# A rewritten beginning: batch 1's tokens loaded at once, its norm shared by VectorE and GpSimd, a fourth unit's queries ahead of the main loop

## The chip, the cores and the metric

The kernel runs on one core of one Trainium2 chip. The metric is the device time of one execution in microseconds, the median of several. A profiled execution gives the time line of each engine: TensorE (PE, with PEld for its weight loads), VectorE (DVE), ScalarE (ACT), GpSimd (POOL) and SyncE (SP), which only issues DMAs. DMAs are also issued by ScalarE and GpSimd, in the order of their own instructions.

## The reference

Two layers of a transformer block over x of 4 batches x 512 tokens x 320, in fp32. Each layer has self attention with 20 heads of 16, cross attention to a context of 1601 tokens of 192, and a gated feed-forward part; each of the three has a layer norm ahead of it and a residual behind it.

```
h1 = _ln(x, n1_g, n1_b)
x = _attn(h1, h1, q1, k1, v1, o1_w, o1_b, heads) + x
h2 = _ln(x, n2_g, n2_b)
x = _attn(h2, context, q2, k2, v2, o2_w, o2_b, heads) + x
h3 = _ln(x, n3_g, n3_b)
a, g = jnp.split(h3 @ ff_w1 + ff_b1, 2, axis=-1)
ff = a * gelu(g) @ ff_w2 + ff_b2
return ff + x
```

`_attn` is softmax(q k^T / 4) v per head, and `_ln` subtracts the mean and multiplies by the reciprocal root of the variance plus 1e-5.

## The kernel before, in words

**Units.** Attention is cut into units: one batch and a group of four heads, so five units per batch and attention (the first unit is batch 0, heads 0 to 3). A unit passes through these stages, and its tiles have these names:

- The norm of its batch, once for five units. VectorE makes the statistics (`st`, `mv`) of four tiles of 128 tokens and starts the reciprocal root by a guess (`root`, four instructions of `guess_root` and three rounds of `better_root`). `plain` writes the rows (`hturned`: x minus mean, times root, three instructions to a tile), TensorE transposes them into `hps`, twelve products against the unit matrix, and `turn` copies them out with gain and bias (`hT`). Behind it `biased` adds the output bias `brow` to x on GpSimd, four additions to a batch.
- `both`: queries and keys of a unit, in two halves of 256 tokens on TensorE (`qkps<-hT,wqk`; the page counts 24 passes for each half). ScalarE copies them to `halves` (for the first unit with VectorE, for others with GpSimd's `split`, a cast and a subtraction, into a high and a low part), and DMAs move them to `kT` and `q`.
- `values`: four chunks of 128 tokens for 8 heads, then four for 12 heads (`vps<-wv,hT`), copied by ScalarE into `vals`.
- The row maxima of the scores: 16 tiles of 128x512 to a unit (`sps<-kT,q`), each reduced by VectorE into `nmax`. `max_pairs` lists them in two deques of four entries, two tiles to an entry, and `round_of` sends what it is given, here four tiles at a time. `max_reduce` and `max_end` finish: three short VectorE instructions, the last of which writes `turned`, and four DMAs to `nrows`.
- The main loop's rounds, four to a unit of self attention: scores once more (`st`), with the row maximum subtracted by a product with `nrows`, the exponential on ScalarE (`pr`), the product with the values (`av`), whose copy `vo` GpSimd adds to `o`.

**Order.** Every engine works off its instructions in the order in which the program was written. In the main loop a planner sets that order: chains of small steps (`norm`, `proj`, `values` and others) with costs and due times in rounds, and `give` adds maxima of coming units. While `start["on"]` is true, at the beginning, nothing is planned: the order is written out by hand in the last part of the kernel, with `run(chain)` for the next step of a chain, `until`, `at_once` (a unit's products and moves) and `round_of`. There the DMAs use the queues of SyncE and ScalarE.

**PSUM.** There are eight banks. `bank` picks the one that is expected to be free first, from running guesses of each engine's time (`written`, `busy`), so TensorE waits for whoever reads the bank that its next product gets.

**DMA counters.** A DMA that lands counts up one of eight landing counters, which all queues share in turn. A DMA waits, before it is issued, for the landing of the one that used its counter before.

The lines of the profile that matter: L182 token loads, L226 bias loads, L523 to L539 root, L563 and L564 statistics, L627 rows, L641 transposes, L647 and L649 `hT`, L620 bias additions, L912 queries and keys, L829 and L830 the split, L880 moves of `kT` and `q`, L1039 and L1021 values, L1080 maxima's products, L1091 their reductions, L1167 and L1175 `turned` and the rows of maxima, L1328 scores, L1338 the exponential, L1354 `av`.

Of the kernel before, what the change touches and what calls it, by code (L numbers as in the profile page):

```python
# [13 lines left out]
ALU = mybir.AluOpType  # L14
# [9 lines left out]
P = 128  # L24
# [54 lines left out]
def kernel(ctx: ExitStack, tc: tile.TileContext, x, context, ws, out):  # L79
# [96 lines left out]

    def load_x(b):

        src = x[b].rearrange("(c p) d -> p c d", p=P)

        def part(t):
            dma(out=xs[b][:, t], in_=src[:, t])  # L182
            loaded[b] = clock["round"] if t == NQ - 1 else 1 << 30

        return [lambda t=t: part(t) for t in range(NQ)]
# [38 lines left out]

    def load_row(t, v):
        dma(out=t, in_=v.rearrange("(o d) -> o d", o=1).to_broadcast([P, D]))  # L226

    def load_bias(l, i):
        if i > 2:
            l, i = l + 1, i - 3  # L230
        if l < L:
            load_row(brow[(3 * l + i) % 2], ws[l][("o1_b", "o2_b", "ff_b2")[i]])

# [298 lines left out]
    def better_root(h, y, z):  # L532


        eng = nc.vector if start["on"] else nc.gpsimd
        eng.tensor_tensor(z, y, y, ALU.mult)
        eng.tensor_tensor(z, z, h, ALU.mult)
        eng.tensor_scalar(z, z, 1.5, None, ALU.add)
        eng.tensor_tensor(y, y, z, ALU.mult)  # L539
# [13 lines left out]
    def add_norm(l, b, i, put, done, due):  # L553
# [68 lines left out]
        def plain(t):  # L622
            if t == 0:
                s["hn"] = one.tile([P, DB, NQ, SLOT], F32, tag="hturned", name="hturned").rearrange("p k t w -> p (k t w)")
            for k, at, n in HK:
                w = n // SLOT
                (nc.vector if start["on"] else nc.gpsimd).tensor_scalar(  # L627
                    s["hn"][:, t * D + at : t * D + at + n].rearrange("p (d k) -> p k d", k=w),
# [7 lines left out]
        def turn(k, at, n):  # L636
            if k == 0:
                place()
            ps = bank("hps")
            for t in range(NQ):  # L640
                nc.tensor.transpose(ps[:n, t * P : (t + 1) * P], s["hn"][:, t * D + at : t * D + at + n], ident)  # L641
            written(0.5, ps)
            busy("act", 0.7, ps)
            to = s["hT"][:n, k].rearrange("p (i t w) -> p t i w", t=NQ, w=SLOT)
            src = ps[:n].rearrange("p (t i w) -> p t i w", t=NQ, w=SLOT)
            if start["on"] and k == 1:
                nc.vector.tensor_scalar(to, src, lng[i][:n, k : k + 1], lnb[i][:n, k : k + 1], ALU.mult, ALU.add)  # L647
# [508 lines left out]
    def max_end(u):  # L1156
# [14 lines left out]
        def rows():  # L1171
            for i in range(P // SLOT):
                part = slice(i * SLOT, (i + 1) * SLOT)
                queue = (nc.sync, nc.scalar, nc.gpsimd, nc.sync)[i] if start["on"] else nc.sync
                queue.dma_start(out=slots[:, :, part], in_=turned[part, :])  # L1175
# [510 lines left out]

    take_rooms(0)
    now(load_x(0))
    now(load_self(0))
    load_bias(0, 0)  # L1690
    load_bias(0, 1)
    now(load_x(1))

    add_norms(0)
    add_proj(units[0])
    warm(5)
    until(lambda: not chains["proj"], "proj")
# [4 lines left out]
    run("proj")  # L1702
    for _ in range(2 * NQ + 2):
        run("norm")
    at_once(units[1])
    add_proj(units[2])
    first = units[0]
    first.pairs = max_pairs(first)
    for chain in ("proj", "proj", "values", None):
        round_of(first.pairs[0].popleft()[1] + first.pairs[1].popleft()[1])  # L1710
        if chain:
            run(chain)

    at_once(units[2])
    run("values")
    max_reduce(first)
    max_end(first)
    loads.extend(load_x(2))
    for fs in (load_out(0, "o1_w"), load_x(3), load_cross(0)):
        loads.extend(fs)  # L1720
    second = units[1]
    second.pairs = max_pairs(second)
    for _ in range(2):
        round_of(second.pairs[0].popleft()[1] + second.pairs[1].popleft()[1])
        run("values")
        run("values")
    start["on"] = False
    clock["credit"] = 0.0

    for u in units[3:SOON]:  # L1730
        add_proj(u)
# [46 lines left out]
```

## Time and profile before

| | us |
|---|---|
| median of 3 runs (lowest, highest) | 2907.66 (2905.47, 2910.71) |
| the profiled execution | 2907.47 |
| its span on the core | 2905.7 |
| mean granted TensorE clock | 0.996 |
| first `st` on TensorE | 44.99 |
| first exponential on ScalarE | 45.99 |

In the timeline a row gives the start, the time from the first start to the last end of the merged instructions, engine, line, operation, tile written and tiles read, the shape, how many, and in brackets the idle time of the engine ahead of it and what ended it. In the windows by stage a row gives the stretch, its length, each engine's busy time with the number of instructions in brackets, the granted TensorE clock, the share of the DMA engines and what they moved.

### The profile page before, as it was taken

What the parts mean: (1) busy time and instruction counts of PE and PEld (TensorE: products, weight loads), DVE (VectorE), ACT (ScalarE), POOL (GpSimd) and SP (SyncE); (2) the same over time, 40 slices, a digit from 0 to 9 for tenths busy, and PEclk for the clock granted to TensorE, in tenths of its full rate; (3) what the DMA queues carried; (4) which work ended last, traced back from release to release, by engine and by line L of the source; (5) the groups of instructions that cost most, each with busy time, mean ns of one, the idle gap of its engine ahead of it and who ended that gap; (6) DMA issues with size and microseconds to landing.
All of it is one profiled execution on the core that took longest, in us unless ns stands there. A gap on an engine that the chain in (4) does not pass through costs nothing.

```text
span 2905.7 us, 83278 instructions
## 1 busy us (share of the span) xinstructions
PE 2847.9 (98%) x35018; PEld 1540.6 (53%) x35018; DVE 1975.7 (68%) x3752; ACT 1949.3 (67%) x4033; POOL 1301.6 (45%) x1409
## 2 busy tenths in 40 slices
PE   8999999999999999999999999999999999999999
PEld 4455555555555555355554555555555555544554
DVE  7776878888888878323257678888878878862221
ACT  3777678888888888501138776788888888893000
POOL 3656345555645555211125653455465564551100
PEclk9999999999999999999999999999999999999999
DMA  3443234232232112200113432222221122122000
GB/s 107 117 118 99 59 83 103 59 80 67 51 93 70 47 54 63 85 17 11 39 44 87 111 97 67 68 64 51 54 73 42 49 73 61 45 68 64 23 22 12
DMA packets 163495, 188.59 MB, mean 65 GB/s; under 512 B 61989, under 2 KB 109105, under 8 KB 163121
## 3 DMA queue, kind: packets, MB, share of 16 engines
q1 hardware_dynamic: 162616, 181.69, 24.6%
q8 instruction: 275, 4.51, 0.6%
q10 hardware_dynamic: 472, 1.58, 0.2%
q14 instruction: 100, 0.81, 0.1%
q0 software_dynamic: 32, 0.00, 0.0%
HBM read 55.76 MB, written 29.36 MB: 29 GB/s over the span
## 4 chain that ended last, share of the span: by engine, by line
PE 87%; DVE 6%; POOL 3%; DMA 1%; issue 1%; ACT 1%; SPq 1%; ACTq 0%; POOLq 0%; DVEq 0%
PE av L1354 22%; PE st L1328 20%; PE fps L1439 10%; PE sps L1080 8%; PE yps L1546 6%; PE vps L1039 5%; PE ops L1254 4%; PE kps L976 3%; PE qkps L912 3%; DVE nmax L1091 3%; PE fps L1499 3%; PE qps L951 2%; DVE pm L1091 2%; PE sps L1105 1%; POOL o L1374 1%
## 5 line engine op out<-in xcount | busy, mean ns | idle before, releaser
L1338 ACT ACTIVATE pr<-st 128x512 f32<-128x512 f32 (+1 forms) x2720 | 1404.9, 603 | 313.2 <-PE st L1328 283.0
L1091 DVE TENSOR_REDUCE pm<-sps 128x1 f32<-128x512 f32 (+1 forms) x1920 | 1148.9, 661 | 235.3 <-PE sps L1080 230.8
L1374 POOL TENSOR_TENSOR o<-o,vo 128x512 f32<-128x512 f32 x576 | 740.7, 1286 | 913.7 <-ACT vo L1373 889.8
L1080 PE MATMUL sps<-kT,q 32*128 32x450 f32 (+1 forms) x4800 | 860.6, 419 | 11.0 <-DMA q<-halves 5.0
L1328 PE MATMUL st<-q,kT 32*128 32x512 f32 (+1 forms) x5120 | 784.4, 419 | 1.9 <-ACT o L1368 1.5
L1354 PE MATMUL av<-pr,vals 128*32 128x512 f32 (+1 forms) x5440 | 735.2, 606 | 28.7 <-ACT pr L1338 6.2
L1328 PEld LDWEIGHTS st<-q,kT 32*128 32x128 f32 (+1 forms) x5120 | 446.6, 180 | 282.1 <-issue 113.6
L1328 PE MATMUL st<-nrows,ones 32*128 32x512 f32 (+1 forms) x2720 | 559.9, 398 | 2.9 <-DMA nrows<-turned 2.8
L1091 DVE TENSOR_REDUCE nmax<-sps 128x1 f32<-128x512 f32 x640 | 397.2, 682 | 117.3 <-PE sps L1080 113.3
L1080 PEld LDWEIGHTS sps<-kT,q 32*128 32x128 f32 x4800 | 429.6, 183 | 64.3 <-ACT pr L1338 11.5
L1373 ACT COPY vo<-av 128x512 f32<-128x512 f32 x576 | 352.5, 612 | 16.6 <-PE av L1354 8.7
L1510 ACT ACTIVATE gl<-fps,b 128x512 f32<-128x512 f32 x80 | 54.8, 687 | 408.8 <-PE fps L1499 299.1
L1439 PE MATMUL fps<-hT,w 128*128 128x512 f32 x640 | 283.1, 597 | 0.0
L1354 PEld LDWEIGHTS av<-pr,vals 128*32 128x32 f32 (+1 forms) x5440 | 111.2, 108 | 302.4 <-DVE pm L1091 187.8
L1328 PEld LDWEIGHTS st<-nrows,ones 32*128 32x128 f32 (+1 forms) x2720 | 262.3, 180 | 12.7 <-DMA nrows<-turned 3.7
L1511 DVE SCALAR_TENSOR_TENSOR hid<-fps,b,gl 128x512 f32<-128x512 f32 x80 | 59.7, 748 | 249.2 <-ACT gl L1510 247.1
L1439 PEld LDWEIGHTS fps<-hT,w 128*128 128x128 f32 x640 | 119.2, 190 | 155.1 <-issue 153.2
L1546 PE MATMUL yps<-w,hid 128*128 128x320 f32 x640 | 175.7, 434 | 0.0
L1546 PEld LDWEIGHTS yps<-w,hid 128*128 128x128 f32 x640 | 120.5, 190 | 56.3 <-ACT gl L1510 5.3
L1254 PEld LDWEIGHTS ops<-wo,aT 112*32 112x32 f32 (+1 forms) x3072 | 98.7, 110 | 67.4 <-issue 33.6
L1254 PE MATMUL ops<-wo,aT 112*32 112x160 f32 (+1 forms) x3072 | 125.7, 301 | 4.2 <-POOL aT L1236 4.0
L1115 DVE TENSOR_REDUCE pm<-sps 128x4 f32<-128x508 f32 x160 | 99.0, 681 | 39.8 <-PE sps L1105 38.8
(89 smaller groups left out, 2449.7 us busy)
## 6 DMA issues: line engine op xcount, KB each, us to landing
kT<-stages SPq DMA_DIRECT2D x80, 400.5 KB
oway<-o SPq DMA_DIRECT2D x80, 256.0 KB
q<-halves SPq DMA_DIRECT2D x80, 256.0 KB
q<-halves SPq DMA_DIRECT2D x27, 512.0 KB
kT<-halves SPq DMA_DIRECT2D x40, 256.0 KB
aT<-oway SPq DMA_DIRECT2D x32, 224.0 KB
rT<-rway SPq DMA_DIRECT2D x32, 224.0 KB
hT<-hturned SPq DMA_DIRECT2D x96, 64.0 KB
```

Of the source, the lines that this page charges most:

```text
L1039: nc.tensor.matmul(ps[f : f + m, :w], lhsT=u.kvT[:n, k, at + f : at + f + m], rhs=wv[:n, k, h0 * DH : h1 * DH], start=(k == 0), stop=(k == ...
L1080: nc.tensor.matmul(own[0][:, :w], lhsT=u.queries(slice(j * SLOT, (j + 1) * SLOT), e, t), rhs=u.kT[j * SLOT : (j + 1) * SLOT, u.k0 + at : u ...
L1091: nc.vector.tensor_reduce(to, own[0][:, :w], AX.X, ALU.max)
L1115: nc.vector.tensor_reduce(u.pm[:, :, j, ns - 1], ps[:, : NQ * w].rearrange("p (t w) -> p t w", w=w)[:, :, :n], AX.X, ALU.max,)
L1254: nc.tensor.matmul(ps[f : f + m, : D // 2], lhsT=aT[:n, k, f * NQ + t * SLOT : f * NQ + t * SLOT + m], rhs=wo[:n, k, cols], start=(k == 0) ...
L1328: nc.tensor.matmul(own[0][:r, :], lhsT=ones[rows, :r] if e == 2 else u.keys(rows, c), rhs=u.rows[rows, :] if e == 2 else u.queries(rows, e ...
L1338: nc.scalar.activation(p[:r], own[0][:r], AF.Exp)
L1354: nc.tensor.matmul(ps[j * SLOT : (j + 1) * SLOT, :], lhsT=columns_of[:r, head : head + SLOT], rhs=pr.pop((c, j))[:r, :], start=True, stop= ...
L1373: nc.scalar.copy(vo, ps)
L1374: nc.gpsimd.tensor_tensor(u.o, u.o, vo, ALU.add)
L1439: nc.tensor.matmul(ps, lhsT=w1[:, k, i * FF + c * P : i * FF + (c + 1) * P], rhs=natural(u.hT[:, k]), start=start, stop=stop,)
L1546: nc.tensor.matmul(ps[:, :D], lhsT=hid[c][:, t * P : (t + 1) * P], rhs=w2[:, c, :], start=(c == 0), stop=(c == NHC - 1),)
```

## The change

Only the beginning is rewritten, and the helpers that it calls, where `start["on"]` or the batch tells them apart.

- Batch 0's four token parts go to SyncE and ScalarE in turn instead of SyncE alone. Batch 1's four, which stood last on SyncE, and the two bias rows follow on ScalarE, ahead of the weights in the program.
- `better_root` on VectorE makes its last two instructions one. This is so for batch 0 and batch 1.
- Batch 1's rows (`plain`) are made by GpSimd instead of VectorE; the first `hT` copy that VectorE did stays with it for batch 0 alone.
- Two warming products more, and three small dummy products between batch 0's first transposes.
- Six of the first unit's value chunks stand right behind the products of the second unit, instead of between and behind the maxima.
- Batch 1's transposes stand ahead of `max_end` of the first unit instead of in the main loop.
- One round of the second unit's maxima stands ahead of the main loop instead of two, and both halves of the fourth unit's queries and keys stand there too.
- The rows of maxima of the first unit go by SyncE and ScalarE in turn; GpSimd issued one of the four before.

On TensorE, from the first unit's products on. Before (the row after these is 24 value products of 12 heads, and then the main loop's first `st`):

```order
L912 MATMUL qkps<-hT,wqk 32x256 x48
L1080 MATMUL sps<-kT_101,q_102 128x512 x8
L912 MATMUL qkps<-hT,wqk 32x256 x12
L1080 MATMUL sps<-kT_101,q_102 128x512 x8
L912 MATMUL qkps<-hT,wqk 32x256 x12
L1080 MATMUL sps<-kT_101,q_102 128x512 x8
L1039 MATMUL vps<-wv_112,hT 32x128 x12
L1080 MATMUL sps<-kT_101,q_102 128x512 x8
L1039 MATMUL vps<-wv_112,hT 32x128 x12
L1080 MATMUL sps<-kT_101,q_103 128x512 x8
L1039 MATMUL vps<-wv_112,hT 32x128 x24
L1080 MATMUL sps<-kT_101,q_103 128x512 x8
```

And of the change, up to the main loop's first `st`:

```order
L920 MATMUL qkps<-hT,wqk 32x256 x48
L1047 MATMUL vps<-wv_112,hT 32x128 x48
L1047 MATMUL vps<-wv_112,hT 32x192 x24
L1088 MATMUL sps<-kT_101,q_102 128x512 x8
L920 MATMUL qkps<-hT,wqk 32x256 x12
L1088 MATMUL sps<-kT_101,q_102 128x512 x8
L920 MATMUL qkps<-hT,wqk 32x256 x12
L1088 MATMUL sps<-kT_101,q_102 128x512 x16
L645 MATMUL hps<-ident,hturned 128x128 x4
L645 MATMUL hps<-ident,hturned 96x128 x8
L1088 MATMUL sps<-kT_101,q_103 128x512 x8
L920 MATMUL qkps<-hT,wqk 32x256 x24
```

The values moved ahead of the first maxima, the transposes (`hps`) and 24 products of the fourth unit came in, and one round of `q_103`, the second unit, went out.

On ScalarE, the program's first instructions are these now; before, they began with the table load, and the token parts and bias rows stood on SyncE. In brackets stands what an instruction waits for, DMAHW being the landing counters:

```order
L182 DMA x_107<-in_x_dram 128x320 x2
L182 DMA x_108<-in_x_dram 128x320 x2
L182 DMA x_108<-in_x_dram 128x320 [waits DMAHW0_49]
L182 DMA x_108<-in_x_dram 128x320 [waits DMAHW2_49]
L226 DMA brow_118<-in_L_xattn_o_b_dram 128x320 [waits DMAHW4_49]
L226 DMA brow_119<-in_L_xattn_o_b_dram 128x320 [waits DMAHW6_49]
L657 ACT_TABLE_LOAD [waits DMAHW5_49,DMAHW3_49]
```

Counters 4 and 6 were used before by batch 1's first two parts, and counters 4 and 6 are used next, on SyncE, by the second of the three key weight loads and the first of the value weights.

On GpSimd, behind the clearing of buffers (x0 and x1 are the tokens of batches 0 and 1). Before:

```order
L620 TENSOR_TENSOR x0_107<-x0_107,brow0_118 128x320 x4
L829 CAST halves_285<-halves_285 128x512
L830 TENSOR_TENSOR halves_285<-halves_285 128x512
L829 CAST halves_380<-halves_380 128x512
L830 TENSOR_TENSOR halves_380<-halves_380 128x512
L1175 DMA nrows0_97<-turned_478 8x4x32
L620 TENSOR_TENSOR x1_108<-x1_108,brow0_118 128x320 x4
```

And of the change, where the last two rows stand four times, and then the third unit's cast and subtraction:

```order
L623 TENSOR_TENSOR x0_107<-x0_107,brow0_118 128x320 x4
L837 CAST halves_288<-halves_288 128x512
L838 TENSOR_TENSOR halves_288<-halves_288 128x512
L630 TENSOR_SCALAR hturned_422<-x1_108,mv_306,root2_321 128x4x32
L630 TENSOR_SCALAR hturned_422<-x1_108,mv_306,root2_321 128x3x32 x2
```

Twelve instructions of rows came in between the second unit's split and the third's, and a DMA issue went out.

The diff, cut to its core:

```diff
-    def load_x(b):
+    def load_x(b, queues=(nc.sync,)):
...
-            dma(out=xs[b][:, t], in_=src[:, t])
+            queues[t % len(queues)].dma_start(out=xs[b][:, t], in_=src[:, t])
...
         eng.tensor_tensor(z, z, h, ALU.mult)
+        if eng is nc.vector:
+            eng.scalar_tensor_tensor(y, z, 1.5, y, ALU.add, ALU.mult)
+            return
...
-                (nc.vector if start["on"] else nc.gpsimd).tensor_scalar(
+                (nc.vector if start["on"] and not b else nc.gpsimd).tensor_scalar(
...
+            idle = bank("wps") if start["on"] and k == 0 and not b else None
             for t in range(NQ):
                 nc.tensor.transpose(ps[:n, t * P : (t + 1) * P], s["hn"][:, t * D + at : t * D + at + n], ident)
+                if idle is not None and t + 1 < NQ:
+                    nc.tensor.matmul(idle[:, :P], lhsT=ident, rhs=fill[:, :P], start=True, stop=True)
...
-            if start["on"] and k == 1:
+            if start["on"] and k == 1 and not b:
...
-                queue = (nc.sync, nc.scalar, nc.gpsimd, nc.sync)[i] if start["on"] else nc.sync
+                queue = nc.scalar if start["on"] and i % 2 else nc.sync
...
-    now(load_x(0))
+    now(load_x(0, (nc.sync, nc.scalar)))
+    now(load_x(1, (nc.scalar,)))
+    load_bias(0, 0, nc.scalar)
+    load_bias(0, 1, nc.scalar)
     now(load_self(0))
-    load_bias(0, 0)
-    load_bias(0, 1)
-    now(load_x(1))
...
-    warm(5)
+    warm(7)
...
-    for _ in range(2 * NQ + 2):
+    for _ in range(NQ + 2):
         run("norm")
+    for _ in range(6):
+        run("values")
     at_once(units[1])
+    for _ in range(NQ):
+        run("norm")
     add_proj(units[2])
...
-    for chain in ("proj", "proj", "values", None):
+    for chain in ("proj", "proj", None, None):
         round_of(first.pairs[0].popleft()[1] + first.pairs[1].popleft()[1])
         if chain:
             run(chain)
 
-    at_once(units[2])
-    run("values")
+    for _ in range(3):
+        run("norm")
     max_reduce(first)
     max_end(first)
+    at_once(units[2])
+    second = units[1]
+    second.pairs = max_pairs(second)
+    round_of(second.pairs[0].popleft()[1] + second.pairs[1].popleft()[1])
+    add_proj(units[3])
+    run("proj")
+    run("proj")
     loads.extend(load_x(2))
...
-    second = units[1]
-    second.pairs = max_pairs(second)
-    for _ in range(2):
-        round_of(second.pairs[0].popleft()[1] + second.pairs[1].popleft()[1])
-        run("values")
-        run("values")
     start["on"] = False
     clock["credit"] = 0.0
 
-    for u in units[3:SOON]:
+    for u in units[4:SOON]:
         add_proj(u)
```

More of the change, by code (lines that the diff above doesn't have):

```diff
@@ L223, in load_columns, with load_row, load_bias @@
         return [lambda c=c: column(*c) for c in chunks]
-    def load_row(t, v):
-        dma(out=t, in_=v.rearrange("(o d) -> o d", o=1).to_broadcast([P, D]))
-    def load_bias(l, i):
+    def load_row(t, v, queue):
+        queue.dma_start(out=t, in_=v.rearrange("(o d) -> o d", o=1).to_broadcast([P, D]))
+    def load_bias(l, i, queue=nc.sync):
         if i > 2:
@@ L231, in load_bias @@
         if l < L:
-            load_row(brow[(3 * l + i) % 2], ws[l][("o1_b", "o2_b", "ff_b2")[i]])
+            load_row(brow[(3 * l + i) % 2], ws[l][("o1_b", "o2_b", "ff_b2")[i]], queue)
     def load_norm(l, i):
@@ L639, in turn @@
             ps = bank("hps")
+            idle = bank("wps") if start["on"] and k == 0 and not b else None
             for t in range(NQ):
                 nc.tensor.transpose(ps[:n, t * P : (t + 1) * P], s["hn"][:, t * D + at : t * D + at + n], ident)
+                if idle is not None and t + 1 < NQ:
+                    nc.tensor.matmul(idle[:, :P], lhsT=ident, rhs=fill[:, :P], start=True, stop=True)
+            if idle is not None:
+                busy("act", 0.0, idle)
             written(0.5, ps)
```

## The prediction

> **What bounds the kernel now.** I read the page's first part, then the windows by stage, then the timeline of the stage that the change rewrites.
>
> ```profile
> PE 2847.9 (98%) x35018; PEld 1540.6 (53%) x35018; DVE 1975.7 (68%) x3752; ACT 1949.3 (67%) x4033; POOL 1301.6 (45%) x1409
> ```
>
> ```profile
> core 0: us, PE busy (x) PEld busy (x) DVE busy (x) ACT busy (x) POOL busy (x), PEclk, DMA share, GB/s
> 13.37:23.79 10.42, 5.44 (x98) 2.88 (x98) 6.23 (x21) 2.67 (x5) 5.14 (x6) 0.85 0.62 185
> 23.79:44.99 21.20, 18.05 (x240) 9.77 (x240) 19.34 (x45) 2.24 (x7) 5.98 (x7) 0.83 0.33 82
> 44.99:90.00 45.01, 43.71 (x647) 23.74 (x643) 29.26 (x54) 32.66 (x68) 15.27 (x14) 1.00 0.35 91
> 90.00:224.00 134.00, 126.07 (x1793) 66.90 (x1793) 98.93 (x202) 100.14 (x202) 82.31 (x104) 0.99 0.45 114
> ```
>
> Over the span TensorE (PE) is the bound: 98% busy. From 44.99 on it is again, 43.71 of 45.01, with VectorE (DVE) at 65%. Before that it is not: from 13.37 to 23.79 it stands half the time, and from 23.79 to 44.99 VectorE is busy for 19.34 of 21.20 us while TensorE issues 240 products, against 647 in the next 45 us. So what the change can win lies ahead of 44.99, where the first `st` stands:
>
> ```profile
> 13.37 5.43 PE L912 MATMUL qkps<-hT,wqk 128*32 128x256 f32 x96
> 17.30 0.66 ACTq L880 DMA_DIRECT2D q<-halves  x1
> 23.79 1.23 PE L1080 MATMUL sps<-kT,q 32*128 32x512 f32 x8 [4.98 <-DMA q<-halves]
> 24.94 2.74 PE L912 MATMUL qkps<-hT,wqk 128*32 128x256 f32 x24
> 25.02 3.39 DVE L627 TENSOR_SCALAR hturned<-x,mv,root 128x128 f32<-128x128 f32 x12
> 28.30 9.65 DVE L1091 TENSOR_REDUCE nmax<-sps 128x1 f32<-128x512 f32 x16
> 29.70 1.50 PE L912 MATMUL qkps<-hT,wqk 128*32 128x256 f32 x24
> 38.41 0.21 DVE L1167 STREAM_TRANSPOSE turned<-nmax 128x32 f32<-128x32 f32 x1
> 38.65 1.42 SPq L1175 DMA_DIRECT2D nrows<-turned  x2
> 40.45 0.96 PE L1080 MATMUL sps<-kT,q 32*128 32x512 f32 x7 [2.23 <-ACT vals L1021]
> 41.17 2.48 DVE L1091 TENSOR_REDUCE nmax<-sps 128x1 f32<-128x512 f32 x4 [0.18 <-PE sps L1080]
> 41.35 3.72 PE L1039 MATMUL vps<-wv,hT 128*32 128x192 f32 x48
> 44.99 0.50 PE L1328 MATMUL st<-q,kT 32*128 32x512 f32 x2
> 45.99 2.28 ACT L1338 ACTIVATE pr<-st 128x512 f32<-128x512 f32 x4 [0.52 <-PE st L1328]
> ```
>
> The reader sees a chain: TensorE waits 4.98 us for the first queries, and 24 products then take 2.74 instead of 1.50 at a lowered clock. VectorE makes batch 1's rows first (3.39) and so starts the 16 maxima only at 28.30, although the first tile was there by about 24.5 (23.79 and the 0.72 from 40.45 to 41.17). TensorE runs out of banks behind it, and waits 2.23 us once more for value copies that stand on ScalarE (ACT) behind its part of the rows of maxima.
>
> **The change, part by part.** First the beginning up to the first products.
>
> ```profile
> 0.73 1.82 SPq L182 DMA_DIRECT2D x<-in_x_dram  x4
> 7.28 0.17 DVE L538 TENSOR_SCALAR root<-root 128x4 f32<-128x4 f32 x1
> 7.49 0.16 DVE L539 TENSOR_TENSOR root<-root,root 128x4 f32<-128x4 f32 x1
> 9.27 3.40 DVE L627 TENSOR_SCALAR hturned<-x,mv,root 128x128 f32<-128x128 f32 x12
> 12.29 1.06 SPq L226 DMA_DIRECT2D brow<-in_L_xattn_o_b_dram  x2
> 17.15 3.32 POOL L620 TENSOR_TENSOR x<-x,brow 128x320 f32<-128x320 f32 x4 [10.73 <-DMA brow<-in_L_xattn_o_b_dram]
> 20.42 0.61 POOL L829 CAST halves<-halves 128x512 fp32r<-128x512 f32 x1
> 21.06 0.17 DVE L523 TENSOR_SCALAR root<-mv 128x4 f32<-128x4 f32 x1
> 21.11 1.26 POOL L830 TENSOR_TENSOR halves<-halves 128x512 f32<-128x512 f32 x1
> 21.27 1.13 DVE L524 TENSOR_SCALAR root<-root 128x4 int32<-128x4 int32 x1
> ```
>
> The fused root drops three instructions of 0.20 (7.28 to 7.49): batch 0's rows start at 9.27 - 0.6 = 8.67. For batch 0's tokens on two queues I take nothing (bounds 0 and 0.9, half of 1.82, since the issues halve but the bytes do not). Against this stands a new neighbour. The bias rows, issued at 12.29, let GpSimd (POOL) add at 17.15, 4.9 us later. Issued now behind six token parts, at about 5 (an estimate: 0.73 and six issues of 0.46 make 3.5, and the issue waits besides for the landing of batch 1's first part), they land near 9.9, when VectorE is amid its rows, and the addition of a tile waits only for that tile's rows and the bias. An addition takes 3.32 / 4 = 0.83, and the row at 21.27 shows what a VectorE `TENSOR_SCALAR` does beside such an operation: 1.13 instead of 0.17, ending as GpSimd's ends. Three tiles can be held: 0 to 2.5 us; I take 1.2, the middle. Products then start 0.6 later than 13.37, at 13.97. The five added dummy products lie in TensorE's idle time before that (warming 7 instead of 5). Two of the key weights' issues on SyncE (SP) wait, through landing counters that the queues share, for the small loads and the first bias row, near 9.9. The products that use them stand 0.5 and more behind 13.97, 4.6 later; the bias rows themselves took 4.9 from issue to use. I cost it at nothing, because weights are not broadcast, and keep 0.3 and the next issue's 0.5 as the bound: 0.8 if that cover is short.
>
> ```profile
> 16.79 0.48 DVE L924 SCALAR_TENSOR_TENSOR halves<-qkps,scales,halves 128x256 f32<-128x256 f32 x1 [0.76 <-ACT halves L923]
> 22.40 0.57 ACTq L880 DMA_DIRECT2D q<-halves  x1
> 27.00:27.50 0.50, 0.50 (x8) 0.00 (x0) 0.50 (x4) 0.00 (x0) 0.00 (x0) 0.50 0.01 0
> 36.27 1.52 PE L1039 MATMUL vps<-wv,hT 128*32 128x128 f32 x48
> ```
>
> Products 5.43, to 19.4. Six value chunks follow at once: four of 8 heads at 1.52 a pair and two of 12 heads, 5.2 in all, to 24.6. The queries' halves end 0.6 after 17.27, at 17.9; the first move took 17.30 to 23.79 (6.5) beside batch 1's tokens, the second, alone, from 22.40 until the traffic stopped, with 0 GB/s from 27.0 on (4.6): here by 22.5 to 24.4. So the 4.98 are filled by values, and maxima start at 24.6 with a warm clock. The second unit's query issue stands on ScalarE behind all six value copies, to about 25; its products come ten us later.
>
> VectorE, from 17.9: statistics 2.53 (18.53 to 21.06), 13 root steps of 0.20, and one hold of 1.0 as at 21.27: 24.0. Maxima follow the first product by 0.72 (40.45 to 41.17): 25.3, and end after 9.65 at 34.95; `turned` 0.67 later, at 35.6 instead of 38.62.
>
> ```profile
> 47.30 1.53 PE L641 MATMUL hps<-ident,hturned 128*128 128x128 f32 x12
> 48.15 2.11 ACT L649 ACTIVATE hT<-hps,lnb,lng 128x512 f32<-128x512 f32 x3
> 51.94 0.74 PE L1080 MATMUL sps<-kT,q 32*128 32x512 f32 x8
> 52.60 2.80 PE L912 MATMUL qkps<-hT,wqk 128*32 128x256 f32 x48
> 62.87 2.14 PE L1039 MATMUL vps<-wv,hT 128*32 128x192 f32 x48
> 102.71 4.41 POOL L627 TENSOR_SCALAR hturned<-x,mv,root 128x128 f32<-128x128 f32 x6
> ```
>
> GpSimd's twelve rows: 24.0 + 2 x 4.41 = 32.8. TensorE's transposes stand behind the maxima and wait tile by tile; the last ends near 33.1, its copy (2.11 / 3) at 33.8. Queued behind them are one round of maxima (0.74) and the fourth unit's products (2.80): 37.3. The clock may fall meanwhile: after 2.23 idle, 48 products took 3.72 instead of 2.14. I take half of 2.74 - 1.50, 0.6: 37.9. ScalarE: after `turned` two row issues (1.42), the third unit's query issue (0.57), and a copy that frees a bank (0.47): 38.1. The later decides; the first exponential stands 1.0 behind the first `st`: 39.1 against 45.99, **6.9 sooner**. Done by then in addition: products 2.80 and transposes 1.53, less a round of maxima 0.74: **3.6**. VectorE owes four maxima more (2.48) to the first rounds of the main loop; its share is 65% there, and I take half, **-1.2** (bounds 0 and 2.5). Sum: 9.3. Behind it TensorE's order differs in a few rows up to 224 us and then not at all; its 7.9 idle us between 90 and 224 may shift by 2 either way, taken as 0.
>
> By the Trainium skill, "TensorE: Matmul & The Clock Gate", section "What's actually happening", the clock falls only after an idle window of about 3.4 us; the wait of 2.23 before the slow products speaks against so long a bound. By that rule nothing is lost while transposes trickle in, and the sum would be 9.9, 2897.8 us.
>
> **The rivals.** (1) GpSimd holds VectorE in full: each of three additions its 0.83, and the root of batch 1 the 0.61 and the 1.26 of the second unit's split instead of 1.0. For it: 1.13 of 1.26 at 21.27. Against: additions that start between VectorE's rows. Price 1.3 + 0.9: gain 7.1, 2900.6. The Trainium skill, "SBUF — State Buffer", section "Who interferes with whom", says just this of the port that the two share, an exclusive lock for a whole instruction. (2) VectorE sets the pace on to the main loop, so that only its own shift counts, 28.30 - 25.3 = 3.0: 2904.7. For it: 19.34 of 21.20 busy, and four maxima more. Against: 29.26 of 45.01 afterwards. (3) Slower: ScalarE's queue comes to wait for GpSimd. The third unit's query issue needs that unit's split, which now stands behind the twelve rows: 32.8 + 0.61 + 1.26 = 34.7, while ScalarE gets there at 37.0. It decides from 2.3 us on, and then delays all exponentials one to one. To be 5.8 slower it needs 17.4 more, 2.2 us a row instead of 0.74: 2913.5. Against: 4.41 for six, beside a busy VectorE. (4) The change does not do what it says: batch 1's tokens, the last two waiting for earlier landings, come no sooner than 19.4. Then root and rows end 1.5 later: 2899.9.
>
> **How the numbers follow.** The sum is made against the profiled execution, 2907.47 (span 2905.7 and 1.8 around it): 2898.2. The median of the runs is 0.2 above it: **2898.4**. About 0.2%, 5.8 us, is what a measurement tells from no change: faster is under 2901.8. Forecast 0.55, with its own range 2894 to 2903.5: at the low end no hold, no fall of the clock, no debt on VectorE (12.3) and some of the 2 us; at the high end a full hold, the full clock, the full debt (6.2) and the 2 us. Rival 1: 0.15, rival 2: 0.18, rival 3: 0.06, rival 4: 0.06. The range reaches to rival 2: 2894 to 2906. Faster: 0.51 of the forecast, 0.08 of rival 1, 0.04 of 2, 0.05 of 4: 0.68. Slower: rival 3 and a remnant of 2, 0.07. Same: 0.25.
>
> **What would show it.** Right: no gap on TensorE between products and maxima; the 16 maxima starting at 25 and ending by 35.5; the first exponential at 38 to 40; the same work after 90 us about 9 us earlier. Wrong: rows of batch 0 that take 5 us or more instead of 3.40 (rival 1); `av` waiting for maxima for over 2 us in the first unit (rival 2); the query issue on ScalarE later than 39 (rival 3); batch 1's statistics later than 19 (rival 4).

## The result, and the profile after

The changed kernel takes 2896.24 us (median of 6 runs, 2894.12 to 2899.26) against 2907.48 (6 runs, 2904.53 to 2910.71) beside it: ratio 0.9961, 95% interval 0.9952 to 0.9971, 11.2 us. The forecast was 2898.4 with a range of 2894 to 2906. Its profiled execution took 2899.26 us, the slowest of the six, with a span of 2897.2, so the two profiles differ by less than the medians: 8.2 us.

The page's first part hardly moves; TensorE is still the bound over the span. After:

```profile
PE 2848.3 (98%) x35028; PEld 1543.2 (53%) x35028; DVE 1972.1 (68%) x3734; ACT 1948.9 (67%) x4033; POOL 1307.5 (45%) x1420
```

Two windows of the beginning, after; the columns are those of the windows shown of before. The first is cut as there:

```profile
13.37:23.79 10.42, 10.42 (x251) 7.37 (x245) 6.68 (x24) 3.79 (x11) 2.94 (x4) 1.00 0.52 130
39.00:42.50 3.50, 3.50 (x48) 2.04 (x40) 1.54 (x3) 1.50 (x4) 0.64 (x1) 0.51 1.01 255
```

From 13.37 to 23.79 TensorE is now busy throughout at full clock (5.44 of 10.42 before, clock 0.85). The second row shows where time is still lost: 3.5 us at half clock behind 39.

The timeline, after:

```profile
8.64 3.39 DVE L630 TENSOR_SCALAR hturned<-x,mv,root 128x128 f32<-128x128 f32 x12
9.67 3.32 POOL L623 TENSOR_TENSOR x<-x,brow 128x320 f32<-128x320 f32 x4 [3.27 <-DVE hturned L630]
12.75 5.44 PE L920 MATMUL qkps<-hT,wqk 128*32 128x256 f32 x96
18.00 4.78 PE L1047 MATMUL vps<-wv,hT 128*32 128x128 f32 x144
19.48 1.28 POOL L838 TENSOR_TENSOR halves<-halves 128x512 f32<-128x512 f32 x1
19.66 1.13 DVE L527 TENSOR_SCALAR root<-root 128x4 int32<-128x4 int32 x1
22.71 0.74 PE L1088 MATMUL sps<-kT,q 32*128 32x512 f32 x8
22.75 8.65 POOL L630 TENSOR_SCALAR hturned<-x,mv,root 128x128 f32<-128x128 f32 x12 [1.98 <-DVE root L539]
23.48 9.66 DVE L1099 TENSOR_REDUCE nmax<-sps 128x1 f32<-128x512 f32 x16 [0.92 <-PE sps L1088]
32.00 1.28 POOL L838 TENSOR_TENSOR halves<-halves 128x512 f32<-128x512 f32 x1
33.60 0.21 DVE L1175 STREAM_TRANSPOSE turned<-nmax 128x32 f32<-128x32 f32 x1
33.84 2.11 ACTq L1183 DMA_DIRECT2D nrows<-turned  x2
36.04 0.60 ACTq L888 DMA_DIRECT2D q<-halves  x1
36.77 0.84 ACT L936 ACTIVATE halves<-qkps,scales 128x256 f32<-128x256 f32 x2 [4.13 <-POOL x L623]
37.29 0.50 PE L1088 MATMUL sps<-kT,q 32*128 32x512 f32 x2 [1.37 <-ACT halves L936]
38.12 2.06 ACT L1346 ACTIVATE pr<-st 128x512 f32<-128x512 f32 x4 [0.51 <-PE sps L1088]
38.77 3.81 PE L1047 MATMUL vps<-wv,hT 128*32 128x192 f32 x48
137.28 0.62 ACT L1376 COPY o<-av 128x512 f32<-128x512 f32 x1
```

Values follow the products at 18.00 without a gap, the maxima start at 23.48 instead of 28.30 with GpSimd's rows beside them, and the first exponential stands at 38.12 instead of 45.99: 7.9 us sooner. The last row is the mark by which the experiments are read: the seventh unit's first value copy on ScalarE. Of the kernel before it reads:

```profile
146.50 0.62 ACT L1368 COPY o<-av 128x512 f32<-128x512 f32 x1
```

So 9.2 us are won by then. The mark is sharper than the time of a whole run. The rest of the span, from the mark to the end, took 2905.7 - 146.50 = 2759.2 us before and 2897.2 - 137.28 = 2759.9 after, and in the runs below it lies anywhere from 2754.5 to 2765.6.

### The profile page after: what moved, and what is told of

It is laid out like the page before. It is cut to its first block, busy times and chain, and to the rows that moved or that the text cites. A ratio compares the mean times of both kernels' runs of the same rounds, so it can differ in the third digit from the quotient of the medians.

```text
span 2897.2 us, 83291 instructions
## 1 busy us (share of the span) xinstructions
PE 2848.3 (98%) x35028; PEld 1543.2 (53%) x35028; DVE 1972.1 (68%) x3734; ACT 1948.9 (67%) x4033; POOL 1307.5 (45%) x1420
## 4 chain that ended last, share of the span: by engine, by line
PE 87%; DVE 6%; POOL 3%; DMA 2%; issue 1%; ACT 1%; SPq 0%; POOLq 0%; ACTq 0%; DVEq 0%
PE av L1362 22%; PE st L1336 20%; PE fps L1447 10%; PE sps L1088 8%; PE yps L1554 6%; PE vps L1047 5%; PE ops L1262 4%; PE kps L984 3%; DVE nmax L1099 3%; PE qkps L920 3%; PE fps L1507 3%; PE qps L959 2%; DVE pm L1099 2%; PE sps L1113 1%; POOL hturned L630 1%
## 5 line engine op out<-in xcount | busy, mean ns | idle before, releaser
L1088 PE MATMUL sps<-kT,q 32*128 32x512 f32 (+1 forms) x4800 | 858.2, 419 | 3.8 <-ACT halves L936 1.4
L1088 PEld LDWEIGHTS sps<-kT,q 32*128 32x128 f32 x4800 | 429.9, 183 | 54.7 <-ACT pr L1346 11.2
L1336 PEld LDWEIGHTS st<-nrows,ones 32*128 32x128 f32 (+1 forms) x2720 | 262.9, 180 | 10.1 <-issue 2.0
```

Source lines behind the costliest of these rows:

```text
L1088: nc.tensor.matmul(own[0][:, :w], lhsT=u.queries(slice(j * SLOT, (j + 1) * SLOT), e, t), rhs=u.kT[j * SLOT : (j + 1) * SLOT, u.k0 + at : u ...
L1336: nc.tensor.matmul(own[0][:r, :], lhsT=ones[rows, :r] if e == 2 else u.keys(rows, c), rhs=u.rows[rows, :] if e == 2 else u.queries(rows, e ...
```

## The experiments

The first three kernels of the table were timed in several runs, each of the others in one, so its time alone tells little; the verdicts rest on the first exponential and on the mark, each read from one profile. The first two rows are two profiles of one program, and they differ by 0.7 us at the first exponential and by 0.9 at the mark: differences below 1 us say little. "Gained" is against the kernel before (45.99 and 146.50), and "lead in between" is how much the gain changed from the first exponential to the mark.

| kernel | first exponential (gained) | mark (gained) | lead in between | time, us |
|---|---|---|---|---|
| changed | 38.12 (7.9) | 137.28 (9.2) | +1.3 | 2896.24, median |
| the same again | 38.85 (7.1) | 136.36 (10.1) | +3.0 | 2894.29, median |
| third unit's moves later | 37.99 (8.0) | 135.50 (11.0) | +3.0 | 2893.66, median |
| rows on VectorE | 41.87 (4.1) | 141.75 (4.8) | +0.6 | 2902.73 |
| values late | 41.31 (4.7) | 138.69 (7.8) | +3.1 | 2898.04 |
| tokens last | 40.75 (5.2) | 138.25 (8.3) | +3.0 | 2896.16 |
| no fourth unit | 38.08 (7.9) | 140.90 (5.6) | -2.3 | 2903.03 |
| straight rows | 39.27 (6.7) | 138.42 (8.1) | +1.4 | 2896.69 |
| before + rows on GpSimd | 46.41 (-0.4) | 146.88 (-0.4) | 0.0 | 2905.52 |
| before + values early | 43.88 (2.1) | 146.56 (-0.1) | -2.2 | 2910.95 |
| the same, filled | 44.93 (1.1) | 145.40 (1.1) | 0.0 | 2907.27 |
| before + rows + values | 42.99 (3.0) | 145.46 (1.0) | -2.0 | 2906.77 |
| the same, filled | 43.16 (2.8) | 145.74 (0.8) | -2.1 | 2913.13 |

### The changed kernel again, and with the third unit's moves later

The first is the changed kernel itself. The second moves the third unit's queries and keys behind the fourth unit's products:

```diff
     max_end(first)
-    at_once(units[2])
     second = units[1]
...
     run("proj")
     run("proj")
+    at_once(units[2])
```

> The changed kernel once more, as it is. Marker in all these runs: the seventh unit's first value copy on ScalarE (o<-av), 146.50 us in the kernel before, 137.28 in the changed one. Theory: the fall of the clock from about 39 to 42.5 us (48 value products in 3.81 instead of 2.14) follows the gap of 1.37 us on TensorE at 35.92 and depends on where that gap lies in a watching window that runs free, so a second profile may show it or not: marker at 137.3 with the fall, 135.6 without. Rival: it belongs to the program and comes each time: 137.3 +- 0.3. Time 2896 +- 2.

> One line moved: the third unit's moves (at_once) stand behind the fourth unit's products, so that ScalarE makes the two copies of the fourth unit ahead of the third unit's query issue. Theory: the gap of 1.37 us on TensorE (35.92 to 37.29) is ScalarE's order; it shrinks to about 0.6, the first exponential comes at 37.4 instead of 38.12, and if the clock stays up the marker comes at 135 to 136 instead of 137.3; time 1 to 3 us less than the changed kernel beside it. Rival A: the rows of maxima land at 36.4 to 36.7 and hold the scores anyway: first exponential at 38.1, no change. Rival B: the third unit's queries, landing 1 us later (42.8), hold its maxima, which now start at 45.04: slower by up to 1 us.

Measured, five rounds each beside nine runs of the kernel before (2906.81): 2894.29 (2892.14 to 2897.34, ratio 0.9953, interval 0.9939 to 0.9966) and 2893.66 (2891.88 to 2899.92, 0.9954, 0.9941 to 0.9966). The two cannot be told apart in time; the 1 to 3 us expected are not to be seen. Windows and timeline of the same program again:

```profile
31.50:35.00 3.50, 3.50 (x26) 1.88 (x29) 3.40 (x8) 1.94 (x3) 3.41 (x5) 0.53 0.00 0
39.50 2.16 PE L1047 MATMUL vps<-wv,hT 128*32 128x192 f32 x48
136.36 0.62 ACT L1376 COPY o<-av 128x512 f32<-128x512 f32 x1
```

Timeline of the kernel with the later moves:

```profile
36.95 0.50 PE L1088 MATMUL sps<-kT,q 32*128 32x512 f32 x2 [0.73 <-ACT halves L936]
135.50 0.62 ACT L1376 COPY o<-av 128x512 f32<-128x512 f32 x1
```

One program, two outcomes. In the first profile the clock fell to half at 39, and the 48 value products took 3.81. In the second it fell at 31.5, while TensorE had slack, and they took 2.16: this run started its maxima 0.7 us later than the first and still stood 0.9 ahead at the mark. So the expectation that the fall is drawn by time, and not set by the program, held; its 135.6 without a fall was 0.8 too early because that run started later. With the moves later, TensorE's wait halves (0.73), no fall is seen, and the mark is 0.9 earlier still; 0.4 of this is again an earlier start of the maxima (23.81 against 24.19). That leaves about 0.5 us for the edit, too little to tell from two profiles.

### Taking one part out of the change

Four parts were taken out one at a time. The fused root, the added dummy products and the queues of the rows of maxima were not, so what each of these brings is not shown by itself.

Batch 1's rows back on VectorE:

```diff
-                (nc.vector if start["on"] and not b else nc.gpsimd).tensor_scalar(
+                (nc.vector if start["on"] else nc.gpsimd).tensor_scalar(
```

> The changed kernel with batch 1's rows back on VectorE; all else stays. Theory: VectorE's chain sets the start: its 16 maxima begin behind 3.4 us of rows at 26.0 instead of 23.48, turned is written at 36.3 instead of 33.8, the first exponential comes 2 us later, at 40.2, marker at 139.3. Rival: ScalarE and TensorE set it: transposes come earlier in their turn, the first exponential stays at 38.1, marker 137.3.

```profile
26.73 9.65 DVE L1099 TENSOR_REDUCE nmax<-sps 128x1 f32<-128x512 f32 x16
42.98 4.07 PE L1047 MATMUL vps<-wv,hT 128*32 128x192 f32 x48
```

The columns are those of the timeline, as in the fences that follow. The maxima start 3.25 us later than in the changed kernel (the rows' 3.39), the first exponential comes 3.8 later where 2 was expected, and on top the clock is at half from 40 to 47: mark 141.75, 2.5 later than the theory had it. No other part, taken out, moves the first exponential so far.

The six value chunks behind the maxima instead of ahead of them:

```diff
-    for _ in range(6):
-        run("values")
     at_once(units[1])
...
+    for _ in range(6):
+        run("values")
     for _ in range(3):
         run("norm")
```

> The changed kernel with the six value chunks behind the first unit's maxima instead of ahead of them. Theory: TensorE stands from 18.2 to 22.4 for the first queries and its clock falls; the maxima start as before the move (23.2 on VectorE), but 4.8 us of values now lie behind them, from about 28.6, and push transposes, the fourth unit's products and the first scores: first exponential at 39.6 to 40, marker 138.8 to 139.3 instead of 137.28. Rival: the values hide in TensorE's waits for banks behind VectorE: 38.1 and 137.3.

```profile
22.46 1.23 PE L1088 MATMUL sps<-kT,q 32*128 32x512 f32 x8 [4.28 <-DMA q<-halves]
30.73 4.80 PE L1047 MATMUL vps<-wv,hT 128*32 128x128 f32 x144
```

The wait for the queries is back (4.28), and the value products, 4.80, stand between the maxima and the transposes. The first exponential is 41.31, 1.3 later than expected; the mark, 138.69, is 0.1 ahead of what was expected, since no fall of the clock follows. The rival, hidden work, is out.

Batch 1's tokens and the bias rows last on SyncE, as before:

```diff
-    now(load_x(0, (nc.sync, nc.scalar)))
-    now(load_x(1, (nc.scalar,)))
-    load_bias(0, 0, nc.scalar)
-    load_bias(0, 1, nc.scalar)
+    now(load_x(0))
     now(load_self(0))
+    load_bias(0, 0)
+    load_bias(0, 1)
+    now(load_x(1))
```

> The changed kernel with the loads in the old order on SyncE alone (batch 0, weights, bias, batch 1). Theory: batch 1's statistics begin at 18.3 instead of 16.56 and its root ends at 24.2 instead of 22.6; the maxima begin at 24.2 instead of 23.48, GpSimd's rows end at 32.9 instead of 31.3; first exponential 38.9, marker 138.2. Rival A: early tokens are worth nothing, because the six value chunks and the queries' landing set the start of the maxima: marker 137.3. Rival B: tokens beside the first queries' move slow that as before (6.5 instead of 5.7 us) and the statistics come at 20: marker 140.

```profile
25.29 9.65 DVE L1099 TENSOR_REDUCE nmax<-sps 128x1 f32<-128x512 f32 x16
32.95 1.61 PE L645 MATMUL hps<-ident,hturned 128*128 128x128 f32 x9 [1.54 <-POOL hturned L630]
35.97 3.86 PE L920 MATMUL qkps<-hT,wqk 128*32 128x256 f32 x48
```

The later root starts the maxima 1.1 to 1.8 us later than in the two profiles of the changed kernel, and TensorE waits 1.54 for GpSimd's rows (0.54 in the changed kernel). The mark agrees with the expectation (138.2), but by luck, since two misses cancel: the first exponential, 40.75, is 1.9 later than expected, and the expected mark had a fall of the clock behind the first exponential in it. This run had its fall earlier, from about 35 to 38, where the fourth unit's products took 3.86 instead of 2.80 and held the first scores up. Batch 0's own rows start at 8.45 here, with its tokens on SyncE alone, against 8.64 and 9.02 in the two profiles of the changed kernel: the second queue bought nothing, as forecast, and batch 1's tokens behind it may even cost batch 0's a little.

Without the fourth unit's queries ahead of the main loop:

```diff
-    add_proj(units[3])
-    run("proj")
-    run("proj")
...
-    for u in units[4:SOON]:
+    for u in units[3:SOON]:
```

> The changed kernel without the fourth unit's products ahead of the main loop (they go back into it). Theory: the first scores then wait for the rows of maxima alone and the first exponential comes at 37.2, 0.9 earlier, while 2.8 us of products come back into the main loop, where TensorE is the bound: marker 139.2 (137.28 + 2.8 - 0.9). Rival: VectorE's maxima pace the first rounds and the products hide there: marker 136.4 to 137.3.

```profile
36.50:43.50 7.00, 6.00 (x60) 3.20 (x60) 2.27 (x4) 2.49 (x5) 0.17 (x1) 0.51 0.58 136
37.28 0.79 PE L1336 MATMUL st<-nrows,ones 32*128 32x512 f32 x2 [3.24 <-DMA nrows<-turned]
39.87 3.92 PE L1047 MATMUL vps<-wv,hT 128*32 128x192 f32 x48
```

The first exponential comes at 38.08 and not at the 37.2 expected: TensorE waits 3.24 for the rows of maxima instead of working, and then runs seven microseconds at half clock. The mark is 140.90, 1.7 later than the theory and 3.6 to 4.5 later than in the changed kernel. The 2.80 of the fourth unit's products filled a wait. That they also kept the clock up is likely, with 7 us at half here against 3.5 in each profile of the changed kernel, but it rests on this one profile.

### Adding one part, or two, to the kernel before

```diff
-                (nc.vector if start["on"] else nc.gpsimd).tensor_scalar(
+                (nc.vector if start["on"] and not b else nc.gpsimd).tensor_scalar(
```

> The kernel before with one part alone: batch 1's rows on GpSimd. Theory: the maxima begin at 24.5 instead of 28.30 and end at 34.2; the first exponential comes at 42.2 instead of 45.99, marker at 143.0 instead of 146.5. Rival: only the wait of 2.23 us at 38.22 goes, since TensorE has values and products in between: first exponential at 43.8, marker 144.3.

Timeline of the kernel before with batch 1's rows on GpSimd:

```profile
34.96 1.26 POOL L830 TENSOR_TENSOR halves<-halves 128x512 f32<-128x512 f32 x1
36.25 0.57 ACTq L880 DMA_DIRECT2D q<-halves  x1
37.18 0.87 PE L1080 MATMUL sps<-kT,q 32*128 32x512 f32 x6 [3.65 <-ACT vals L1021]
```

Nothing is won; the theory and its rival fell alike. Maxima start at 25.43 and `turned` is 2.4 us sooner, but the third unit's split now ends at 36.2, behind GpSimd's rows; the query issue on ScalarE waits for it (33.81 before); the value copies behind the issue wait too, and TensorE waits 3.65 us for a bank. This is the wait of the forecast's third rival: in the old order nothing covers it, and it eats all that the earlier maxima bring. In the changed kernel the split ends at 33.28 (32.00 + 1.28), and the issue comes at 36.04, behind the rows of maxima: 2.8 us of slack, and no value copies behind it.

The values early, alone, and then with two dummy products behind each of four later rounds of maxima:

```diff
+    for _ in range(6):
+        run("values")
     at_once(units[1])
...
-    for chain in ("proj", "proj", "values", None):
+    for chain in ("proj", "proj", None, None):
...
-    run("values")
     max_reduce(first)
...
-        run("values")
-        run("values")
```

> The kernel before with one part alone: the six value chunks right behind the second unit's products. Theory: the 4.98 us of waiting are filled and the clock stays up; VectorE still begins its maxima at 28.3 and writes turned at 38.6, but nothing stands behind it on TensorE: first scores near 39.5, the rows of maxima land at 41, first exponential at 41.8 instead of 45.99, marker at 142.3 instead of 146.5. Rival: VectorE sets the pace all the way, so that filled time on TensorE is lost again: marker 145 or later.

> The kernel before with the six value chunks moved ahead of the maxima, and two dummy products of 512 columns behind each of four later rounds of maxima. Moved alone, the values brought the first exponential from 45.99 to 43.88, but the seventh unit's first value copy stayed at 146.56 (146.50 before), and the TensorE clock stood at 0.50 from 28.5 to 49. Theory: the value products between the maxima had kept the clock up, and the lost clock ate the gain. With the dummies the clock is 1.00 from about 32 to 49, the first exponential stands at 43.3 to 43.9, since the rows of maxima still land at 43, and the copy at 144 to 145. Rival: the clock costs nothing there, because VectorE sets the pace; then the copy stays at 146.0 to 146.6 whatever the clock.

Windows and timeline, values early alone:

```profile
28.50:49.00 20.50, 19.46 (x97) 11.06 (x101) 17.72 (x33) 4.66 (x8) 5.94 (x7) 0.51 0.20 48
33.37 7.40 PE L1080 MATMUL sps<-kT,q 32*128 32x512 f32 x32
45.67 2.82 PE L641 MATMUL hps<-ident,hturned 128*128 128x128 f32 x12
```

And with the dummies:

```profile
33.00:49.00 16.00, 15.55 (x103) 7.16 (x95) 14.28 (x26) 4.44 (x8) 5.95 (x7) 0.99 0.25 61
42.01 1.98 PE L435 MATMUL wps<-fill,ident 128*128 128x512 f32 x4
46.24 1.53 PE L641 MATMUL hps<-ident,hturned 128*128 128x128 f32 x12
```

Alone, the values bring the first exponential 2.1 us forward and the mark not at all: the expectation of 142.3 fell, and the rival's 145 or later came. For 20.5 us the clock stands at half. What TensorE has there is mostly scores at VectorE's pace, eight passes for every four reductions, 2.4 us; the page calls it busy (19.46), because the ends of waiting matmuls are modelled, but 97 passes in 20.5 us is little work. The value products, which had stood between the maxima, had been holding the clock: with dummies in their place it is 0.99 from 33 on, the transposes take 1.53 instead of 2.82, and the lead at the first exponential (1.1) is kept to the mark. The last dummies run from 42.01 to 43.99 and the first `st` comes behind them, at 43.92, so the exponential comes 1.1 later than without them and the mark falls 0.4 short of the expected range, still clear of the rival's.

Both parts together, and both filled:

> The kernel before with two parts of the change: batch 1's rows on GpSimd and the six value chunks ahead of the maxima, nothing else. Alone, the rows brought the copy to 146.88 and the values to 146.56, against 146.50. Theory: each part alone hits the wait that the other removes (with the rows alone, ScalarE's value copies stand behind the third unit's query issue, which waits for GpSimd's rows; with the values alone, VectorE makes the rows first). Together: maxima start at 25 to 25.5, turned at 35.3 to 36, first exponential at 39.5 to 41, copy at 142 to 143.5, with the clock at 0.50 for part of 35 to 47. Rival: the two do not help each other, copy at 146 or later.

> The same two parts, and two dummy products behind each of four later rounds of maxima. Theory: first exponential as without the dummies, within 0.7, the clock at 1.00 from 30 on, copy 1.5 to 2.5 earlier than without, 140 to 141.5. Rival: copy within 0.5 of the one without the dummies, or later because the dummies stand in the way.

Timeline and windows of the two parts together:

```profile
35.20 0.21 DVE L1167 STREAM_TRANSPOSE turned<-nmax 128x32 f32<-128x32 f32 x1
35.91 0.57 ACTq L880 DMA_DIRECT2D q<-halves  x1
36.52 3.04 SPq L1175 DMA_DIRECT2D nrows<-turned  x2
42.20 0.79 PE L1328 MATMUL st<-nrows,ones 32*128 32x512 f32 x2 [3.15 <-DMA nrows<-turned]
34.00:47.50 13.50, 10.00 (x39) 5.42 (x38) 8.55 (x17) 3.65 (x6) 5.81 (x8) 0.51 0.29 72
```

And filled:

```profile
30.00:41.50 11.50, 9.38 (x46) 3.38 (x45) 11.25 (x21) 0.00 (x0) 9.82 (x13) 1.00 0.32 77
42.36 0.79 PE L1328 MATMUL st<-nrows,ones 32*128 32x512 f32 x2 [2.98 <-DMA nrows<-turned]
```

`turned` is there at 35.20, 3.2 us sooner than before and about as expected, but the first exponential only at 42.99, 2 us behind the latest time expected, and the mark at 145.46, between theory and rival. Of the rows of maxima, four DMAs of 4 KB, three are now issued just behind the third unit's moves of 512 and 256 KB (35.91), and TensorE can use the rows only 7 us after `turned`; in the kernel without the fourth unit, where they stand ahead of those moves, it took 3.6 (33.71 to 37.28). SyncE's two issues take 3.04 us instead of 1.42 in the kernel before; what the second one waits for, the trace does not show. The fourth row, which GpSimd issues, shows the effect by itself: here it stood just ahead of the moves (35.83) and landed 2.2 us after its issue; with the rows on GpSimd alone it stood just behind them (36.56, the moves at 36.25) and took 5.2. In the kernel before the moves were issued at 33.81 and 4.8 us ahead of the rows of maxima, and out of the way. The dummies hold the clock up to 41.5, but TensorE still waits 2.98 for the rows, and the clock falls then: here the rival was right, 145.74 against 145.46. The theory that the two parts only cover each other's wait was therefore incomplete: the third piece, as far as these runs show, is that in the change `max_end` stands ahead of the third unit's moves, which the forecast had in its order but did not price. Exchanging those two alone was not run. The Trainium skill, "DMA: Bandwidth & Descriptors", section "Issuing engines are not separate DMA queues", says that transfers of all engines share the same DMA engines and interleave; the 7.0 against 3.6 agree with it.

### The rows beside GpSimd's additions

```diff
-                    s["hn"][:, t * D + at : t * D + at + n].rearrange("p (d k) -> p k d", k=w),
-                    xb[:, t, at : at + n].rearrange("p (k d) -> p k d", k=w),
+                    s["hn"][:, t * D + at : t * D + at + n] if l == 0 and b == 0 else s["hn"][:, t * D + at : t * D + at + n].rearrange("p (d k) -> p k d", k=w),
+                    xb[:, t, at : at + n] if l == 0 and b == 0 else xb[:, t, at : at + n].rearrange("p (k d) -> p k d", k=w),
```

> The changed kernel, but batch 0's rows are written in the order of the tokens' columns instead of permuted by heads, so what is computed for batch 0 in the first layer is not the reference's; nothing else is changed. In the changed kernel the twelve rows took 3.39 us beside four additions on GpSimd (from 9.67 for 3.32), as long as alone, while a short TENSOR_SCALAR of the root took 1.13 instead of 0.17 beside one GpSimd operation. Theory: what GpSimd holds is a VectorE instruction with straight operands, and the permuted ones pass it. Straight rows then take longer beside the additions than 3.39, 4.5 us or more from first to last, with single rows of 0.6 and more that end with an addition. Rival: rows are never held, and straight ones take 3.4 or less.

Timeline with straight rows, and the group of that line (its shortest, median and longest, in ns):

```profile
8.64 4.67 DVE L630 TENSOR_SCALAR hturned<-x,mv,root 128x128 f32<-128x128 f32 x12
9.56 0.88 POOL L623 TENSOR_TENSOR x<-x,brow 128x320 f32<-128x320 f32 x1 [3.16 <-DVE hturned L630]
L630 DVE TENSOR_SCALAR hturned<-x,mv,root x12: 317/334/874, 8.6 to 13.0; 128x96 f32<-128x96 f32 x8, 128x128 f32<-128x128 f32 x4
```

And of the changed kernel, permuted rows beside the same additions:

```profile
L630 DVE TENSOR_SCALAR hturned<-x,mv,root x12: 391/396/405, 8.6 to 11.6; 128x96 f32<-128x96 f32 x8, 128x128 f32<-128x128 f32 x4
```

Straight rows are quicker where nothing holds them (median 0.33 against 0.40), and beside the additions some take up to 0.87; the twelve take 4.67 instead of 3.39. Permuted ones run through, none over 0.41. The theory held, in one run: what GpSimd's addition holds is the straight form. The products start 1.1 us later for it (13.81), and the mark is at 138.42.

## Why the prediction was right, and where it was not

**What bounds.** Right for what the traces can place: of the 9.2 us at the mark, 7.9 lie ahead of the first exponential, and the views named showed what could be won there, VectorE's rows ahead of the maxima and TensorE's wait for the queries. That the sum of 9.3 met 9.2 so closely is in part luck. The first exponential came 1.0 sooner than forecast, the moved work brought 0.6 more, and the clock took 1.7 behind it; the second profile of the same program has 10.1.

**The hold of batch 0's rows: the step that was mis-sized.** The forecast took 1.2 us (bounds 0 and 2.5) from a root instruction that took 1.13 instead of 0.17. It measured 0: 3.39 for the rows beside four additions, and products at 12.75, where 13.97 was forecast. The row that was used as the price was of another form, straight and short; the run with straight rows shows the hold that was feared, 1.3 us. The Trainium skill, "SBUF — State Buffer", section "Who interferes with whom", says that a `tensor_scalar` *can* take the shared port pair when its operands meet conditions; the two runs agree that some forms take it and others do not (0.87 and 0.40 beside the same addition), but which condition the permuted rows miss, they do not show. Rival 1, which applied the lock to all rows, fell. For batch 1's root the one hold of 1.0 came as forecast (19.66, beside 19.48).

**Values in the wait.** Right: no gap between products and maxima, warm. The products of the maxima start at 22.71 instead of 24.6: 1.2 from the hold, most of the rest because the value products took 4.7 and not 5.2.

**VectorE and GpSimd.** Maxima from 23.48 (forecast 25.3), `turned` written by 33.81 (35.6), GpSimd's rows done at 31.4 (32.8): each earlier, mostly by the same 1.2 us.

**ScalarE.** It decided, as forecast: TensorE goes on at 37.29, when the first copy of the halves (from 36.77) has freed a bank. But two rows of maxima took 2.11 to issue and not 1.42, and short gaps between issues and copy added 0.3. This gave back 1.0 of the 1.8 by which `turned` came sooner than forecast; the first exponential followed TensorE by 0.83 instead of 1.0. So it came at 38.12 against 39.1, 7.9 us sooner and not 6.9.

**From the first exponential to the mark.** The forecast was 3.6 of moved work less 1.2 of VectorE's debt, 2.4. In the four kernels that have the moved work and whose clock did not fall behind the first exponential it is 3.0, 3.0, 3.0 and 3.1; in the two where the 48 value products behind it took 3.81, it is 1.3 and 1.4. So with 3.6 moved, the debt was half as large, 0.6; that split is worked out and not measured apart.

**The clock.** The forecast took 0.6 ahead of the first exponential. In the profile of the changed kernel the loss stood behind it, 3.81 - 2.14 = 1.7, after a wait of 1.37; the same program again had it where it cost nothing, and the kernel with the later moves did not have it. Over these three profiles the term is a draw between 0 and 1.7, and 0.6 happens to be their mean. With it the sum closes: 7.9 + 3.0 - 1.7 = 9.2 for the first profile, 7.1 + 3.0 = 10.1 for the second. By the Trainium skill, "TensorE: Matmul & The Clock Gate", section "What's actually happening", the window of about 3.4 us runs freely, which agrees with 39.0 to 42.5 and 31.5 to 35.0 here; that it takes an idle window of that length does not agree with the wait of 1.37, nor with the fall at 31.5, ahead of which TensorE had waited 0.5.

**From the mark to the end.** The forecast took 0, give or take 2. Between the two profiles it was -0.7 (2759.2 against 2759.9), but the medians differ by 11.2, and by 12.5 in the second comparison, while the lead at the mark was 9.2 and 10.1. Over the six profiled runs with the old beginning, or with one or two parts put into it, the rest took 2760.6 on average (2759.2, 2756.8, 2762.6, 2760.1, 2759.5, 2765.6), over the eight with the new one, whole or with a part taken out, 2757.5 (2754.5 to 2760.1). Where the scatter comes from shows in windows further on. The changed kernel's first profile:

```profile
165.00:200.00 35.00, 31.20 (x448) 16.71 (x444) 20.24 (x41) 20.91 (x41) 22.69 (x32) 0.95 0.50 128
270.00:285.00 15.00, 12.83 (x180) 7.05 (x172) 5.80 (x14) 5.95 (x14) 4.27 (x4) 0.89 0.28 66
330.00:345.00 15.00, 14.24 (x164) 6.99 (x164) 11.04 (x20) 9.30 (x20) 6.30 (x5) 0.89 0.18 55
```

In the kernel with the later moves all three windows have a clock of 1.00, and in the same program again the second alone is low (0.89). The fall at 39 cost 1.7 us; what each of these costs was not measured apart. Whether the new beginning makes such falls rarer, which would be the missing 2 us, or the draw went its way, stays open.

**The rivals.** (2), VectorE sets the pace up to the main loop, fell: the maxima start 4.8 sooner (23.48 against 28.30), and the mark comes 9.2 sooner. (3), ScalarE waiting for GpSimd, did not happen, but the rows added alone show that it does in the old order. (4) fell: batch 1's statistics start at 16.6 and its root at 19.08.

## What to carry to other kernels

The parts of this change were worth 1 to 5 us each at the mark when one was taken out of it, and the two that were added alone were worth nothing, because each moved the wait to the next queue or gave it to the clock: GpSimd's split and ScalarE's copies behind it for the rows, the clock for the values. Added together they met one wait more, small DMAs that land late behind two large ones. When an engine is made faster at a start, list what is issued next on every queue and what it stands behind, and price the order of transfers as well as that of instructions. Filler work between the steps of a slower engine may be what holds TensorE's clock: before it is moved away, look at what is left in that stretch and at the granted clock there.

## What the runs showed of the hardware that was not expected

- The clock fell without any long wait of TensorE: with scores alone at VectorE's pace, about a third of the time in work (0.74 of every 2.4 us), it went to half at 34 us in the kernel with two parts added, and it stayed there for 20.5 us in the one with the values early; two dummy products for every eight score passes held it at 0.99 to 1.00.
- Low stretches, read to half a microsecond, lasted 3.5 us (two profiles of the changed kernel, at different places), 7 (no fourth unit), 13.5 and 20.5: about once, twice, four and six times 3.4.
- A VectorE `TENSOR_SCALAR` with permuted operands is not held by a GpSimd addition, while the same work with straight operands is: at most 0.47 us an instruction in six profiles of the changed kernel and its variants, against up to 0.87 in the one run with straight rows.
- Two issues of 4 KB on SyncE took 3.04 us right behind large moves, against 1.42 otherwise, and a row issued by GpSimd landed 5.2 us after its issue behind them, against 2.2 just ahead of them.
